# A top-2 mixture of experts on one core: six fixed blocks per expert, or five in twos with shared half blocks

## The chip, the cores and the metric

The kernel runs on one core of a Trainium2 chip. The metric is the device time in microseconds (us) of one execution. Work is done by TensorE (PE in the profile, its weight loads PEld), VectorE (DVE), ScalarE (ACT), GpSimd (POOL) and by DMA queues, most of which SyncE (SP) issues.

## The reference, cut to what matters

Two layers over 2708 tokens of 256 channels, float32. Each layer is a graph attention over an adjacency matrix followed by a feed-forward part; in layer 0 this holds a causal attention too. Both end in a mixture of 8 experts, of which every token uses its best two:

```python
probs = softmax(flat @ router_w.T)              # (2708, 8)
tp, ti = top_k(probs, 2); tp = tp / (tp.sum(-1) + 1e-9)
for e in range(8):                              # hidden width 682
    hh = silu(flat @ w1[e].T) * (flat @ w3[e].T)
    out = out + weights[:, e:e+1] * (hh @ w2[e].T)
```

That is 5416 pairs of token and expert in each layer. How many of them an expert gets depends on the data; the mean is 677.

## The kernel before, in words

The program is `network`: `first` (graph attention, causal attention, routing of layer 0), `experts_blocks(0)`, `second` (graph attention and routing of layer 1), `experts_blocks(1)`. The routing writes each token's row of 268 floats (channels, token number, 8 gates) to a table `xs` in DRAM by an indirect DMA, once for each of its two experts. Expert e owns the rows from e * CAP on and is filled from the front; rows that nobody writes are those that `clear` has put there before (channels and gates 0, a token number beyond the last).

`experts_blocks` works on fixed blocks of P = 128 rows: NB = 6 for every expert, 768 rows, whether they are full or not. For a block (e, j) `fetch` loads the rows into a tile `xt` (SP's queue), `front` transposes them on PE and ACT copies them back as `xT`. `up` (line 2008) multiplies with w1 and w3: the weights are PE's stationary operand, a chunk of 128 hidden units at a time, and the 128 tokens of `xT` move through. The last 42 of the 682 hidden units of both matrices share one chunk (`REST`, `HIGH`). ACT applies SiLU, DVE the product, and the result `hT` has the hidden units on the partitions. `down` (line 2028) takes `hT` as the stationary operand and lets w2 (256 columns) move through, six chunks into one bank of PSUM `y`. DVE scales with the gate (`ys`), and `add_rows` (line 609) adds the rows to their tokens in DRAM by an indirect DMA on POOL's queue. `down` of a block comes after `up` of the next one, and `front` runs two blocks ahead.

The weights of an expert (some 2.1 MB, six DMAs in `load_expert`, line 1967) lie in one of three `rooms`; the next expert's are loaded while the one before last is no longer needed. The first two experts are loaded before the phase.

Not all blocks are worked in `experts_blocks`. A few whose rows are known to be complete early (`EARLY`) run inside `first` and `second`, and the last two of expert 7 in layer 0 (`LATE`) run at the start of `second`, beside the loading of X: tiles of X up to `LATE_T` are loaded ahead of them, the others after. So 43 blocks are left for the phase of layer 0 and 44 for that of layer 1. At the end, flags tell whether the data fit all these assumptions (`missed`, `counts`); if not, a general version of the network runs again (`network_any`).

Two things set the order of instructions. In `first` and `second` a planner (`Plan`) with durations and due times written by hand issues the steps, each engine in that order. In `experts_blocks` the framework's scheduler puts the instructions in each engine's queue: an instruction goes there when its operands and buffers are free by the scheduler's own reckoning, those that stand first in the code going first. So a queue need not have the order of the code. On the chip each queue is worked in order.

Of the kernel before, what the change touches and what calls it, by code (L numbers as in the profile page):

```python
# [10 lines left out]
F32 = mybir.dt.float32  # L11
# [27 lines left out]
NB = 6  # L39
# [4 lines left out]
LATE, LATE_T = ((7, 4), (7, 5)), 12  # L44
# [101 lines left out]
def adj_ffn_kernel(ctx, tc, x, adj, vecs, bias_rows, tab, w_gnn0, w_gnn1, wqkv, wo,  # L146
# [371 lines left out]
    def some_blocks(add, layer, blocks, fetched, needs, weights, xs, acc, new, named, rank):  # L518

        joins = []  # L520
        for k, (e, j, before) in enumerate(blocks):
# [62 lines left out]
            def join(v=v):  # L584
                add_rows(layer, acc, v["ys"], v["xt"])
# [23 lines left out]
    def add_rows(layer, acc, ys, xt):  # L609

        nc.gpsimd.indirect_dma_start(  # L611
            out=acc[:, :], out_offset=bass.IndirectOffsetOnAxis(ap=xt[:, C:C + 1].bitcast(I32), axis=0),
            in_=ys, in_offset=None, compute_op=ALU.add,
            **(dict(bounds_check=N - 1, oob_is_err=False) if layer else {}))
# [795 lines left out]
    def second(X, XB, xs0, x1, x2, sd, mb, xs, arena, load_weights):  # L1410
# [9 lines left out]
        with ExitStack() as s:  # L1420
# [93 lines left out]
            for a, b in zip((0,) + ends, ends):  # L1514
                loads.append(add("SP", 0.45 * (b - a), lambda a=a, b=b: nc.sync.dma_start(
                    out=X[:, a:b, :], in_=x1[a * P:b * P, :].rearrange("(t p) c -> p t c", p=P)),
                    late, rank=-9.0, lands=2.0 if 0 < a < LATE_T else 14.0 if a == 0 else 7.0))
# [449 lines left out]
    def load_expert(room, w1, w3, w2, e):  # L1967
        cut = NF * P
        a, b, c, d = weights_at(room)
        nc.gpsimd.memset(c, 0.0)  # L1970
        nc.gpsimd.memset(d[:, NF, :], 0.0)
        w1v, w3v = (w[:, e, :].rearrange("(k p) h -> p k h", p=P) for w in (w1, w3))
        nc.sync.dma_start(out=a, in_=w1v[:, :, :cut])
        nc.sync.dma_start(out=b, in_=w3v[:, :, :cut])
        nc.sync.dma_start(out=c[:, :, :REST], in_=w3v[:, :, cut:])
        nc.sync.dma_start(out=c[:, :, HIGH:], in_=w1v[:, :, cut:])
        nc.sync.dma_start(out=d[:, :NF, :], in_=w2[e, :cut, :].rearrange("(k p) c -> p k c", p=P))
        nc.sync.dma_start(out=d[:REST, NF, :], in_=w2[e, cut:, :])

    def experts_blocks(layer, w1, w3, w2, xs, acc, arena):  # L1980
# [4 lines left out]

        with ExitStack() as s:
            keep = s.enter_context(tc.tile_pool(name=f"bkeep{layer}", bufs=1))
            hTs = [keep.tile([P, NHC, P], F32, name=f"hT{i}") for i in range(3)]
            for hT in hTs:
                nc.gpsimd.memset(hT[:, NF, :], 0.0)  # L1990
            rooms = [arena[:, :WE], arena[:, WE:], keep.tile([P, WE], F32, name="room")]

            with tc.tile_pool(name=f"slot{layer}", bufs=2) as sp, \
                    tc.tile_pool(name=f"bpu{layer}", bufs=2, space=PSUM) as pu, \
                    tc.tile_pool(name=f"bpt{layer}", bufs=1, space=PSUM) as pt_:

                def fetch(e, j):
                    xt = sp.tile([P, ROW], F32, tag="xt", name="xt", bufs=5)
                    row = e * CAP + j * P
                    after_all(nc.sync.dma_start(out=xt, in_=xs[row:row + P, :]), xs)  # L2000
                    return xt

                def front(xt):
                    xT = sp.tile([P, KC, P], F32, tag="xT", name="xTs", bufs=3)
                    transpose_row(xT, xt, P, pt_, V_LN2 if layer == 0 else None)
                    return xT

                def up(k, w, xT):

                    pp = pu.tile([P, 3 * GW // P, P], F32, tag="pp", name="pup")  # L2010
                    for n in range(2 * NF + 1):
                        if n < 2 * NF:
                            wn, to = w[n // NF][:, :, n % NF * P:(n % NF + 1) * P], P
                        else:
                            wn, to = w[2], HIGH + REST
                        for c in range(KC):
                            nc.tensor.matmul(pp[:to, n, :], wn[:, c, :], xT[:, c, :],  # L2017
                                             start=(c == 0), stop=(c == KC - 1))
                    hT = hTs[k % len(hTs)]
                    sl = sp.tile([P, NF, P], F32, tag="sl", name="sl")  # L2020
                    nc.scalar.activation(sl, pp[:, :NF, :], AF.Silu)  # L2021
                    nc.vector.tensor_tensor(hT[:, :NF, :], sl, pp[:, NF:2 * NF, :], ALU.mult)  # L2022
                    sr = sp.tile([P, P], F32, tag="sr", name="sr")
                    nc.scalar.activation(sr[:REST], pp[HIGH:HIGH + REST, 2 * NF, :], AF.Silu)
                    nc.vector.tensor_tensor(hT[:REST, NF, :], sr[:REST], pp[:REST, 2 * NF, :], ALU.mult)
                    return hT

                def down(e, w, hT, xt):
                    y = pt_.tile([P, C], F32, tag="y", name="y")
                    for n in range(NHC):  # L2030
                        nc.tensor.matmul(y, hT[:, n, :], w[3][:, n, :], start=(n == 0), stop=(n == NHC - 1))  # L2031
                    ys = sp.tile([P, C], F32, tag="ys", name="ys", bufs=3)
                    nc.vector.tensor_scalar(ys, y, xt[:, C + 1 + e:C + 2 + e], None, ALU.mult)  # L2033
                    add_rows(layer, acc, ys, xt)

                done = [b[:2] for b in EARLY[layer]] + list(() if layer else LATE)
                blocks = [(e, j) for e in range(NE) for j in range(NB) if (e, j) not in done]
                xt = [fetch(*blocks[k]) for k in range(3)]
                nxt = [front(xt[k]) for k in range(2)]
                last = None  # L2040
                for k, (e, j) in enumerate(blocks):
                    if k + 3 < len(blocks):
                        xt.append(fetch(*blocks[k + 3]))
                    if j == (2 if e else 3) and e + 2 < NE:
                        load_expert(rooms[(e + 2) % 3], w1, w3, w2, e + 2)
                    if (e, j) == (2, 0):

                        pc = pt_.tile([P, C], F32, tag="y", name="pc")
                        nc.tensor.matmul(pc[:, :NE], allones, hsum[:, NT, :], start=True, stop=True)
                        nc.vector.tensor_tensor(counts[:, layer, :], pc[:, :NE], part, ALU.subtract)  # L2050

                        tests = [(e, t, (j + 1) * P, ALU.is_lt) for e, j, t in EARLY[layer]]
                        if layer == 0:
                            tests.append((LATE[0][0], LATE_T, LATE[0][1] * P, ALU.is_gt))
                        for i, (e_, t, places, test) in enumerate(tests):
                            at = (i + 1) * NE
                            nc.tensor.matmul(pc[:, at:at + 1], allones, hsum[:, t, e_:e_ + 1], start=True, stop=True)
                            to = i + layer * (FLAGS - len(EARLY[1]))
                            nc.vector.tensor_scalar(missed[:, to:to + 1], pc[:, at:at + 1], float(e_ * CAP + places), None, test)
                    if layer == 1 and (e, j) == (3, 0):  # L2060
                        raise_flag(keep, lambda name: pt_.tile([P, C], F32, tag="y", name=name))
                    xT = nxt[k]
                    we = weights_at(rooms[e % 3])
                    hT = up(k, we, xT)
                    if k + 2 < len(blocks):
                        nxt.append(front(xt[k + 2]))
                    if last is not None:
                        down(*last)
                    last = (e, we, hT, xt[k])
                down(*last)  # L2070
# [59 lines left out]
    counts = resid.tile([P, 2, NE], F32, name="counts")  # L2130
    missed = resid.tile([P, FLAGS], F32, name="missed")
# [5 lines left out]
    def raise_flag(fp, bank):  # L2137
        bad = fp.tile([P, 8, NT], F32, name="bad")
        for row in (3, 6, 7):
            nc.vector.memset(bad[:, row, :], 0.0)  # L2140
        nc.vector.tensor_copy(bad[:, 7, :FLAGS], missed)
        nc.vector.tensor_scalar(bad[:, 6, :2 * NE].rearrange("p (a e) -> p a e", a=2), counts, float(NB * P),
                                None, ALU.is_gt)
        nc.vector.tensor_scalar(bad[:, 0, :], norms, BOUND, None, ALU.is_gt)
# [75 lines left out]
```

## Time and profile before

| | |
|---|---|
| median of 3 runs | 1554.26 us (1552.09 to 1555.1) |
| the profiled execution | 1553.19 us, its span 1551.5 us |
| mean granted TensorE clock | 0.982 |
| PE busy | 1468.3 us (95%) in 8988 instructions |
| PE weight loads busy | 1153.4 us (74%) |
| DVE, ACT, POOL busy | 740.9, 551.9, 533.0 us |
| read from and written to DRAM | 87.38 and 61.55 MB |

The span is the time from the first to the last instruction; 1.7 us of the execution lie around it. A line of the timeline gives the start in us, the time that a run of like instructions took, the engine, the line of the kernel, the operation, the tiles written and read, shapes, and how many there were; in brackets stands the idle time before and what ended it. Shapes of a matmul are contraction rows * stationary columns, then partitions x moving columns.

### The profile page before, as it was taken

What the parts mean: (1) busy time and instruction counts of PE and PEld (TensorE: products, weight loads), DVE (VectorE), ACT (ScalarE), POOL (GpSimd) and SP (SyncE); (2) the same over time, 40 slices, a digit from 0 to 9 for tenths busy, and PEclk for the clock granted to TensorE, in tenths of its full rate; (3) what the DMA queues carried; (4) which work ended last, traced back from release to release, by engine and by line L of the source; (5) the groups of instructions that cost most, each with busy time, mean ns of one, the idle gap of its engine ahead of it and who ended that gap; (6) DMA issues with size and microseconds to landing.
All of it is one profiled execution on the core that took longest, in us unless ns stands there. A gap on an engine that the chain in (4) does not pass through costs nothing. (4 is left out here: it accounts for less than half of the span.)

```text
span 1551.5 us, 23359 instructions
## 1 busy us (share of the span) xinstructions
PE 1468.3 (95%) x8988; PEld 1153.4 (74%) x8988; DVE 740.9 (48%) x1450; ACT 551.9 (36%) x1068; POOL 533.0 (34%) x695
## 2 busy tenths in 40 slices
PE   6878899999999999999999899999999999999995
PEld 5633433433437899999999678888778999999995
DVE  6688999966685122222221554867753222222221
ACT  3577766754544111111111453443332111111110
POOL 6677679681163222222222300030444222222221
PEclk9899999999999999999999999999999999999998
DMA  7689767620013332333222850541414333332211
GB/s 261 214 274 316 238 231 252 193 67 8 7 54 94 96 75 53 90 90 90 36 36 33 177 117 1 132 111 61 149 58 109 79 87 88 74 87 50 34 34 17
DMA packets 168029, 165.68 MB, mean 107 GB/s; under 512 B 81384, under 2 KB 148264, under 8 KB 165200
## 3 DMA queue, kind: packets, MB, share of 16 engines
q1 hardware_dynamic: 142582, 134.26, 28.5%
q0 software_dynamic: 21056, 26.24, 9.9%
q10 hardware_dynamic: 4270, 3.58, 0.7%
q8 instruction: 73, 1.20, 0.3%
q14 instruction: 48, 0.39, 0.1%
HBM read 87.38 MB, written 61.55 MB: 96 GB/s over the span
## 5 line engine op out<-in xcount | busy, mean ns | idle before, releaser
L2017 PEld LDWEIGHTS pup<-xTs,arena 128*128 128x128 f32 x2772 | 319.2, 191 | 3.7 <-ACT xTs L283 0.7
L2017 PE MATMUL pup<-xTs,arena 128*128 128x128 f32 x2772 | 321.2, 276 | 0.5 <-ACT xTs L283 0.5
L2022 DVE TENSOR_TENSOR hT<-sl,pup 128x640 f32<-128x640 f32 x87 | 71.5, 821 | 451.4 <-ACT sl L2021 451.4
L2021 ACT ACTIVATE sl<-pup 128x640 f32<-128x640 f32 x87 | 61.2, 703 | 504.5 <-PE pup L2017 499.3
L1578 PE MATMUL po<-hb,PT 128*128 128x257 f32 (+2 forms) x968 | 225.9, 388 | 3.7 <-DVE PT L1571 3.7
L1578 PEld LDWEIGHTS po<-hb,PT 128*128 128x128 f32 (+2 forms) x968 | 176.3, 188 | 42.6 <-issue 11.6
L2031 PE MATMUL y<-arena,hT 128*128 128x256 f32 x756 | 173.8, 380 | 0.6 <-DVE ys L2033 0.6
L1100 ACT ACTIVATE e<-stt 128x1024 f32<-128x1024 f32 (+1 forms) x132 | 125.4, 986 | 93.4 <-PE stt L1094 69.0
L1139 DVE TENSOR_TENSOR es<-es,e 128x1024 f32<-128x1024 f32 x104 | 138.0, 1327 | 29.4 <-ACT e L1100 22.9
L2031 PEld LDWEIGHTS y<-arena,hT 128*128 128x128 f32 x756 | 138.8, 190 | 17.2 <-DVE ys L2033 1.0
L611 POOL DMA_INDIRECT out<-ys,xt x44 | 68.3, 1553 | 231.1 <-DVE ys L2033 228.1
L611 POOL DMA_INDIRECT acc<-ys,xt x43 | 67.1, 1560 | 225.8 <-DVE ys L2033 223.9
L1094 PE MATMUL stt<-qT,kT 64*128 64x512 f32 (+1 forms) x528 | 132.9, 614 | 4.6 <-ACT e L1100 4.5
L1805 POOL DMA_INDIRECT xs<-XR,place x88 | 93.7, 1065 | 92.2 <-DVE mk L1565 41.2
L2017 PE MATMUL pup<-xTs,room 128*128 128x128 f32 (+1 forms) x1056 | 123.8, 276 | 0.0
L2017 PEld LDWEIGHTS pup<-xTs,room 128*128 128x128 f32 (+1 forms) x1056 | 121.9, 190 | 1.2
L1120 PE MATMUL o<-e,V 128*64 128x512 f32 (+1 forms) x528 | 122.4, 586 | 0.0
L1556 ACT ACTIVATE E<-sb,dcol 128x768 f32<-128x768 f32 (+1 forms) x88 | 75.1, 858 | 104.4 <-DVE PT L1571 104.0
L1094 PEld LDWEIGHTS stt<-qT,kT 64*128 64x128 f32 x528 | 44.6, 187 | 77.2 <-issue 62.1
L1120 PEld LDWEIGHTS o<-e,V 128*64 128x64 f32 x528 | 32.9, 136 | 68.6 <-issue 52.6
L2033 DVE TENSOR_SCALAR ys<-y,xt 128x256 f32<-128x256 f32 x87 | 42.1, 484 | 54.2 <-PE y L2031 54.2
L2031 PE MATMUL y<-room,hT 128*128 128x256 f32 x288 | 66.1, 379 | 0.0
(275 smaller groups left out, 1922.0 us busy)
## 6 DMA issues: line engine op xcount, KB each, us to landing
arena<-in_adj SPq DMA_DIRECT2D x21, 1354.0 KB, 7.9
arena<-in_w SPq DMA_DIRECT2D x36, 640.0 KB, 4.6
mb<-mb SPq DMA_DIRECT2D x44, 352.0 KB, 2.4
xs<-none SPq DMA_DIRECT2D x16, 804.0 KB, 11.1
xt<-xs SPq DMA_DIRECT2D x87, 134.0 KB, 2.1
room<-in_w SPq DMA_DIRECT2D x12, 640.0 KB, 5.5
acc<-X SPq DMA_DIRECT2D x21, 128.0 KB, 1.7
out<-X SPq DMA_DIRECT2D x21, 128.0 KB, 1.7
```

The source lines that it names most:

```text
L611: nc.gpsimd.indirect_dma_start(out=acc[:, :], out_offset=bass.IndirectOffsetOnAxis(ap=xt[:, C:C + 1].bitcast(I32), axis=0), in_=ys, in_off ...
L1094: nc.tensor.matmul(st[:r, g, c0(sb):], kT[a:b, sb * P:sb * P + r], qT[a:b, t0 + (sb == t0 + 1):t0 + 2, :, :], start=True, stop=True)
L1100: nc.scalar.activation(e[:r, :, c0(sb):], v[sb, "st"][:r, :, c0(sb):], AF.Exp, scale=1.0 / HD ** 0.5)
L1120: nc.tensor.matmul(v["o"][g * HD:(g + 1) * HD, c:], V[:r, sb, g * HD:(g + 1) * HD], v[sb][:r, g, c:], start=(n + i == 0), stop=(n + i == t ...
L1139: nc.vector.tensor_tensor(es, es, v[sb][:r, :, c:], ALU.add)
L1556: nc.scalar.activation(e[:q, :n], sb[:q, i0:i1], AF.Exp, bias=dcol[:q, j:j + 1], scale=SLOPE - 1.0)
L1578: nc.tensor.matmul(v["po", i][:r, :F], v["PT", j][:q, a:a + r], hb[:q, j, :], start=(j == 0), stop=(j == NT - 1))
L1805: i = nc.gpsimd.indirect_dma_start(out=xs[:, :], out_offset=bass.IndirectOffsetOnAxis(ap=at, axis=0), in_=src, in_offset=None)
L2017: nc.tensor.matmul(pp[:to, n, :], wn[:, c, :], xT[:, c, :], start=(c == 0), stop=(c == KC - 1))
L2021: nc.scalar.activation(sl, pp[:, :NF, :], AF.Silu)
L2022: nc.vector.tensor_tensor(hT[:, :NF, :], sl, pp[:, NF:2 * NF, :], ALU.mult)
L2031: nc.tensor.matmul(y, hT[:, n, :], w[3][:, n, :], start=(n == 0), stop=(n == NHC - 1))
```

## The change

- `NB` is 5: five fixed blocks per expert, 640 rows. They are worked in units of two (`fetch`, `front`, `up`, `down` take a list): `up` moves 256 columns (two blocks) through each stationary chunk of weights and hands each chunk to ACT and DVE by itself; `down` runs five chunks of each block and then the rest chunk of both, the second on partitions 64 and up, with w2's last rows loaded twice for it. The fifth block of an expert is a unit alone.
- Rows beyond 640 go in half blocks of 64 rows, ten for all experts together (`MORE`). `table` works out on DVE from the counts whose they are and where they begin. Two half blocks make one unit: one on partitions 0 to 63, the other on 64 to 127, with the weights of their experts in two more rooms, loaded by register (`register`, `bass.ds`). There the tokens are the stationary operand (64 columns each) and the weights move; `turn_halves` transposes the result one unit later, and `down_halves` follows another unit later. Their units stand ahead of the experts 2 to 6, and after each but the last the two rooms are loaded anew.
- `clear` writes rows 512 to 1024 of an expert, not 0 to 768. A room that has been in use is not zeroed again. `xt` has nine buffers, not five; PSUM has five banks for `up`, two for `y`.
- `LATE` is the blocks 3 and 4 of expert 7, not 4 and 5, and `LATE_T` 10, not 12; the planner's landing times of three X loads differ.
- The flags ask for 512 to 960 rows per expert and at most ten half blocks.

So `experts_blocks` has 35 blocks (14 units of two, 7 of one) and 5 shared units in layer 0, and 36 blocks (15 and 6) and 5 shared units in layer 1.

```diff
-NB = 6
+NB = 5
+HALF_B = 64
+MORE = 10
+LEAST, MOST = 512, 960
-LATE, LATE_T = ((7, 4), (7, 5)), 12
+LATE, LATE_T = ((7, 3), (7, 4)), 10
...
     def clear(xs, e):
-        nc.sync.dma_start(out=xs[e * CAP:e * CAP + NB * P, :].rearrange("(b p) c -> p b c", p=P),
-                          in_=none.unsqueeze(1).to_broadcast([P, NB, ROW]))
+        at, n = e * CAP + LEAST, MOST + HALF_B - LEAST
+        nc.sync.dma_start(out=xs[at:at + n, :].rearrange("(b p) c -> p b c", p=P),
+                          in_=none.unsqueeze(1).to_broadcast([P, n // P, ROW]))
...
-    def load_expert(room, w1, w3, w2, e):
+    def load_expert(room, w1, w3, w2, e, used=False):
-        nc.gpsimd.memset(c, 0.0)
-        nc.gpsimd.memset(d[:, NF, :], 0.0)
+        if not used:
+            nc.gpsimd.memset(c, 0.0)
+            nc.gpsimd.memset(d[:, NF, :], 0.0)
...
+            w1v, w3v = (w[:, bass.ds(e, 1), :].rearrange("(k p) o h -> p k (o h)", p=P) for w in (w1, w3))
+            w2v = w2[bass.ds(e, 1)].rearrange("o h c -> (o h) c")
...
+        for q in (0, HIGH):
+            nc.sync.dma_start(out=d[q:q + REST, NF, :], in_=w2v[cut:, :])
...
+                        if e is None:
+                            for h in range(2):
+                                row = register(tab[0:1, 1, j + h:j + h + 1], NE * CAP - HALF_B)
+                                after_all(nc.sync.dma_start(out=xt[h * HALF_B:(h + 1) * HALF_B, :],
+                                                            in_=xs[bass.ds(row, HALF_B), :]), xs)
...
+                def up(k, w, xT, B):
+                    for n in range(NHC):
+                        pp = pu.tile([P, 2, 2, P], F32, tag="pp", name="pup")
...
+                                nc.tensor.matmul(pp[:to, i, :B, :], wn[:, c, :], xT[:, c, :B, :],
+                                                 start=(c == 0), stop=(c == KC - 1))
...
+                def down(e, w, hT, xts):
+                    ys = [bank() for _ in xts]
+                    for b, y in enumerate(ys):
+                        for n in range(NF):
+                            nc.tensor.matmul(y, hT[:, n, b, :], w[3][:, n, :], start=(n == 0), stop=False)
+                    for b, y in enumerate(ys):
+                        part_ = slice(HIGH * b, HIGH * (b + 1)) if len(ys) > 1 else slice(0, P)
+                        nc.tensor.matmul(y, hT[part_, NF, b, :], w[3][part_, NF, :], start=False, stop=True)
...
+                def up_halves(w, xT, xt, pair):
+                    big, gate, both = (pu.tile([P, 2 * C], F32, tag="pp", name="pup") for _ in range(3))
+                    cut = (NF - 1) * P
+                    for to, at, i, a, b in ((big, 0, 0, 0, cut), (both, 0, 0, cut, cut + P), (both, P, 1, cut, cut + P),
+                                            (both, 2 * P, 2, 0, HIGH + REST), (gate, 0, 1, 0, cut)):
                         for c in range(KC):
+                            for q, wh in zip(halves, w):
+                                nc.tensor.matmul(to[q, at:at + b - a], xT[:, c, 0, q], wh[i][:, c, a:b],
+                                                 start=(c == 0), stop=(c == KC - 1))
...
+                def down_halves(w, hT, xt, gk):
+                    y = bank()
                     for n in range(NHC):
+                        for q, wh in zip(halves, w):
+                            nc.tensor.matmul(y[q, :], hT[:, n, 0, q], wh[3][:, n, :], start=(n == 0), stop=(n == NHC - 1))
...
+                    add_rows(acc, yw[halves[0]], xt[:HALF_B, C:C + 1], layer)
+                    add_rows(acc, yw[halves[1]], upper[:HALF_B], layer)
...
+                for e in range(NE):
+                    left = [(e, j) for j in range(NB) if (e, j) not in done]
+                    if 2 <= e < 2 + MORE // 2:
+                        units.append([(None, 2 * (e - 2))])
+                    units += [left[i:i + 2] for i in range(0, len(left), 2)]
...
+                    if k == 2 or k > 2 and units[k - 3][0][0] is None and more_asked < MORE:
+                        for room in more_rooms:
+                            load_expert(room, w1, w3, w2, register(tab[0:1, 0, more_asked:more_asked + 1], NE - 1), more_asked > 1)
+                            more_asked += 1
+                    if k + 2 < len(units):
+                        xt.append(fetch(units[k + 2]))
...
+                    for f, *args in downs.get(k, ()):
+                        f(*args)
```

More of the change, by code (lines that the diff above doesn't have):

```diff
@@ L584, in join @@
             def join(v=v):
-                add_rows(layer, acc, v["ys"], v["xt"])
+                add_rows(acc, v["ys"], v["xt"][:, C:C + 1], layer)
             r = rank + k
@@ L2037, in experts_blocks @@
[L2037 to L2050, printed above, removed]
+                        for q, wh in zip(halves, w):
+                            nc.tensor.matmul(y[q, :], hT[:, n, 0, q], wh[3][:, n, :], start=(n == 0), stop=(n == NHC - 1))
@@ new lines, in experts_blocks @@
+                own = keep.tile([P, MORE // 2, NE], F32, name="mown")
+                tab = keep.tile([P, 2, MORE], I32, name="mtab")
+                pc = bank()
+                nc.tensor.matmul(pc[:, :NE], allones, hsum[:, NT, :], start=True, stop=True)
+                nc.vector.tensor_tensor(counts[:, layer, :], pc[:, :NE], part, ALU.subtract)
+                done = [b[:2] for b in EARLY[layer]] + list(() if layer else LATE)
+                units = []
+                for e in range(NE):
[3 more added lines that the diff above has]
+                    units += [left[i:i + 2] for i in range(0, len(left), 2)]
@@ new lines, in experts_blocks @@
+                xt = [fetch(u) for u in units[:2]]
+                nxt = [front(x) for x in xt[:2]]
+                asked, more_asked = 1, 0
+                turns, downs = {}, {}
+                for k, unit in enumerate(units):
+                    e = unit[0][0]
+                    if k == 0 or e is not None and e + 2 < NE and asked < e + 2 and units[k - 1][0][0] == e:
+                        asked += 1
+                        load_expert(rooms[asked % 3], w1, w3, w2, asked, asked > 2)
+                    if k == 1:
+                        table()
+                    if k == 2 or k > 2 and units[k - 3][0][0] is None and more_asked < MORE:
[4 more added lines that the diff above has]
+                        xt.append(fetch(units[k + 2]))
+                    if unit[0] == (2, 2):
+                        pc = bank()
@@ L2055, in experts_blocks @@
                         for i, (e_, t, places, test) in enumerate(tests):
-                            at = (i + 1) * NE
-                            nc.tensor.matmul(pc[:, at:at + 1], allones, hsum[:, t, e_:e_ + 1], start=True, stop=True)
+                            nc.tensor.matmul(pc[:, i:i + 1], allones, hsum[:, t, e_:e_ + 1], start=True, stop=True)
                             to = i + layer * (FLAGS - len(EARLY[1]))
[L2059 to L2065, printed above, removed]
+                            nc.vector.tensor_scalar(missed[:, to:to + 1], pc[:, i:i + 1], float(e_ * CAP + places), None, test)
+                    if layer == 1 and unit[0] == (3, 0):
+                        raise_flag(keep, lambda name: bank())
+                    if e is None:
+                        we = [weights_at(room) for room in more_rooms]
+                        hid, gk = up_halves(we, nxt[k], xt[k][0], unit[0][1] // 2)
+                        turns[k + 1] = (k, hid, we, xt[k][0], gk)
+                    else:
+                        we = weights_at(rooms[e % 3])
+                        hT = up(k, we, nxt[k], len(unit))
+                        downs.setdefault(k + 1, []).append((down, e, we, hT, xt[k]))
+                    if k in turns:
+                        of, hid, we, x, gk = turns[k]
+                        downs.setdefault(k + 1, []).append((down_halves, we, turn_halves(of, hid), x, gk))
+                    if k + 2 < len(units):
                         nxt.append(front(xt[k + 2]))
[L2067 to L2070, printed above, removed]
+                    for f, *args in downs.get(k, ()):
+                        f(*args)
+                for f, *args in downs[len(units)]:
+                    f(*args)
     dram = ctx.enter_context(tc.tile_pool(name="dram", bufs=1, space=bass.MemoryType.DRAM))
```

163 lines of the change are left out of this document (125 added, 38 removed).

## The prediction

> **What bounds the kernel now.** I read busy time by stretch first, then the timeline of one block, then the waits. The change lives in the two expert phases (508 to 846 us and 1194 to 1536 us), so these rows decide (span; busy us of PE, PEld, DVE, ACT, POOL; PEclk, DMA share, GB/s):
>
> ```profile
> core 0: us, PE busy (x) PEld busy (x) DVE busy (x) ACT busy (x) POOL busy (x), PEclk, DMA share, GB/s
> 600.00:700.00 100.00, 100.00 (x754) 95.99 (x753) 20.59 (x39) 19.39 (x52) 21.47 (x17) 1.00 0.35 78
> 1300.00:1400.00 100.00, 100.00 (x755) 96.02 (x754) 20.46 (x42) 15.73 (x38) 21.39 (x17) 1.00 0.36 83
> ```
>
> PE never pauses, at a granted clock of 1.00; the others are a fifth busy, the DMA engines a third. In 500 to 850 us PE waited three times in all:
>
> ```profile
> PE pt L278 <- DMA xt<-xs: 1.7, 1, 1.7
> PE pup L2017 <- ACT xTs L283: 0.5, 1, 0.5
> ```
>
> So in these phases time is the number of PE instructions by their spacing. The timeline of one block (start, us, instructions):
>
> ```profile
> 625.83 5.06 PE L2017 MATMUL pup<-xTs,arena 128*128 128x128 f32 x44
> ...
> 630.73 0.38 PE L278 MATMUL pt<-ident,xt 128*128 128x128 f32 x2
> ...
> 630.95 2.76 PE L2031 MATMUL y<-room,hT 128*128 128x256 f32 x12
> ...
> 633.54 0.72 PE L2017 MATMUL pup<-xTs,arena 128*128 128x128 f32 x5
> ```
>
> A float32 matmul is two instructions (22 give x44). From start to start: 44 of 128 columns take 4.90 us, 111.4 ns each; 2 transposes 0.22; 12 of 256 columns 2.59, 215.8 ns each. A block is 7.71 us; 43 + 44 blocks are 670.8 us.
>
> The attention stage shows matmuls in halves of the array side by side:
>
> ```profile
> 330.58 1.94 PE L1120 MATMUL o<-e,V 128*64 128x512 f32 x8
> 332.44 1.99 PE L1094 MATMUL stt<-qT,kT 64*128 64x512 f32 x8
> 334.36 1.98 PE L1020 MATMUL pm<-wq_sb,hTt 128*128 128x512 f32 x4
> 336.27 1.94 PE L1120 MATMUL o<-e,V 128*64 128x512 f32 x8
> ```
>
> Eight half-array instructions take 1.86 us (column halves) or 1.92 (row halves), four of the whole array 1.91: two halves cost one whole. At 215.8 / 256 ns a column four of 512 would be 1.73, so a group pays 0.13 to 0.19 us, I take 0.19, for going into another tiling and out.
>
> **The change, part by part.**
>
> Pairs. `up` has 44 instructions of 256 columns for two blocks: 9.50 us, before 9.80. `front` 0.44 as before. `down` 20 x 0.2158 = 4.32, and the rest chunk as two row halves side by side, 2 x 0.2158 + 0.19 = 0.62. A pair is 14.88 us against 15.42, 0.54 less. Layer 0 has 14 pairs and 7 singles, layer 1 15 and 6. A single stays 7.71.
>
> For pairs the Trainium skill promises more: its page "TensorE: Matmul & The Clock Gate", section Back-to-back issue gap, gives 81 ns a matmul at 128 columns and 131 at 512, so a pair's `up` would need far less than twice a block's. The rows above (111.4 and 215.8 ns) say nearly twice, and I go by them.
>
> Shared units. `up_halves`: 5 groups x 2 chunks x 2 passes = 20 side-by-side slots: 8 of 512 at 0.432, 8 of 128 at 0.111, 4 of 106 at 0.11, 4.79 us, with the tiling 4.98. `turn_halves` 6 transposes 0.66, `front` 0.22, `down_halves` 12 x 0.2158 + 0.19 = 2.78. Together 8.64 us, ten times.
>
> Sum: 29 x 14.88 + 13 x 7.71 + 10 x 8.64 = 618.1 us, **52.7 less**.
>
> A rule of the Trainium skill speaks against this: "TensorEngine Tiling (Array Packing)", section Key Properties, says that changing the tiling mode drains TensorE. The excess of 0.19 us a group agrees in kind; if each of the 98 switches laid bare the whole 380 ns of a 256-wide instruction in place of its 216, that would be 16 us where my terms hold 9.
>
> Scatter-adds. The tail shows their spacing:
>
> ```profile
> 1533.38 2.86 PE L2031 MATMUL y<-arena,hT 128*128 128x256 f32 x12 [0.58 <-DVE ys L2033]
> 1533.60 1.55 POOL L611 DMA_INDIRECT out<-ys,xt  x1 [5.94 <-DVE ys L2033]
> ...
> 1538.19 1.55 POOL L611 DMA_INDIRECT out<-ys,xt  x1 [3.04 <-issue]
> ```
>
> Each waits for the one before to land: 4.6 us apart. Inside a phase that hides: 7 adds an expert cycle (5 blocks, 2 halves) are 32 us beside 8.64 + 2 x 14.88 + 7.71 = 46 us of PE. At the end it shows. With T the end of the last pair's `down`, its adds start at T + 0.6 and T + 5.2, and the last single's, whose matmuls end at T + 3.1, at T + 9.8: 6.7 us after PE. Before it was 1.95 us (PE ends at 1536.24). **+4.7** at the end, and as much ahead of the X load that opens `second`; there 15.4 us of late blocks cover part (PE waited 4.9 us behind that load before): 0 to 4.7, I take **+3**.
>
> Output banks. `down_halves` comes straight after a pair's `down` and needs a bank that DVE is still reading; the 0.58 us above is that wait. 10 x 0 to 0.58: **+3**.
>
> Weights. Ten more experts a layer, 2.1 MB each. SP's rows show an old load threaded between fetches:
>
> ```profile
> 620.54 0.38 SPq L1973 DMA_DIRECT2D room<-in_w  x1
> 622.98 0.32 SPq L2000 DMA_DIRECT2D xt<-xs  x1
> 623.39 0.39 SPq L1974 DMA_DIRECT2D room<-in_w  x1
> ...
> 630.85 0.34 SPq L2000 DMA_DIRECT2D xt<-xs  x1
> 633.30 0.37 SPq L1977 DMA_DIRECT2D room<-in_w  x1
> ```
>
> The code issues a load in one piece; the queue has its pieces where their buffers come free, with fetches between. A load alone moved from 491 to 499 us:
>
> ```profile
> GB/s 0 0 0 0 82 92 133 195 287 328 399 410 410 410 410 410 348 399 369 397 283 203 179 194 215 73 0 66 209 340 356 373 385 385 352 189 29 0 0 0
> ```
>
> 8 us each, three a cycle, 24 of 46 us: room enough, and the w1 and w3 pieces have some 35 us between one shared unit and the next. Register loads (one TENSOR_LOAD of the flag on SP: 487 ns), four a cycle, lie on an SP that mostly waits. Cost from 0 (all hidden) to the second rival's price; I take 0.5 us per cycle, **+4** with the phases' slower start (four blocks to fetch ahead).
>
> What waits behind an SP instruction that blocks is the next fetch, and behind that PE's transposes.
>
> The rest. `table`, some 20 small DVE instructions, lies beside 15 us of the first pair on a DVE a fifth busy; bare it would be 4 us a layer. Per-chunk SiLU and product (256 columns, by the 484 ns of L2033) fit within a chunk's 1.73 us. Dropped `load_expert` memsets free POOL, which is not late. `clear` writes 4 rather than 6 blocks an expert: DVE waited 18.8 us on `X<-hd,ix` in that stage, some of it for bandwidth; 0 to -5, **-1**. LATE's earlier tiles: 0, +-3.
>
> From the profiled execution's 1553.2 (span 1551.5): -52.7 + 4.7 + 3 + 3 + 4 - 1 = -39, so 1514.2; the median of runs is 1.1 above that execution: **1515 us**.
>
> **Rivals.**
>
> Scatter-adds become the bound (faster still). More weight traffic slows them: landing was 3.6 to 5.4 us, with 0.8 for the hand-over (4.6 less the median 3.8) 6.2 at worst, and 6.6 each fills the cycle. At 7.0 a cycle is 49 us, +2.8 x 12 cycles = 34: **1549**. With partial weight waits of 2 to 3 us at ten reloads (+20, 1535) I give this family 0.18.
>
> Slower: SP's queue keeps the order of the code. Then the last piece of a room's load waits for `down_halves`, and behind it stand the second room's load and the next pair's fetch. From there: 1.4 us to start (490.14 to some 491.5 in the load above), 2 for the piece (497 to 499), 8 for the room, 1 for the rows, 12.4; PE has only a single's `up`, 4.9, to do before the transposes: 7.5 us, four times. At the first load two rooms stand ahead: 20.4 less 9.5. That is 41 us a layer, +82: **1597**. It decides from 39 / 10 = 3.9 us per reload. For it: SP did stand at a load's first piece, waiting for `pup`, up to 19.9 us; against: the threaded rows. Chance 0.13, with all prices from 42 us up.
>
> Slower too: column halves with different weights run one after the other: (4.79 + 2.59) x 10 = +74, 1589. L1120's two halves also differ in both operands and ran side by side: 0.03.
>
> It does not do what it says: an expert over 960 rows, or over ten half blocks, would run the network again, above 3000 us. Routing the reference's inputs by its own formulas gives 598 to 745 rows an expert and 8 half blocks in each layer: nil.
>
> **Numbers.** Likeliest case 0.62 (1504 to 1526). Range 1503 to 1550: it adds the first rival. A measurement of this kernel tells 0.2%, 3.1 us. Faster 0.8, within 0.04 (rivals' prices that land there), slower 0.16.
>
> **What would show it.** `up` of a pair at 44 instructions 216 ns apart; shared units with slots of two half-array instructions, some 5 us for `up_halves`; PE near 100% in both phases, which shrink by some 26 us each; last scatter-adds 4.6 us apart after PE's end. I am wrong if PE shows waits of several us for `xt`, `more` or `room` near shared units, if spacing in `up_halves` is twice as wide, or if scatter-adds hold `xt` so long that fetches come late.

## The result and the profile after

The changed kernel takes 1555.16 us (median of 20 runs, 1547.01 to 1560.91); the kernel before, run beside it, takes 1552.66 us (1550.25 to 1556.18). The ratio is 1.0012, 95% interval 1.0000 to 1.0024: no gain of the 39 us that were forecast, and at most 0.24% slower. The profiled execution of the changed kernel took 1552.57 us, its span is 1550.8 us, and the mean granted clock is 0.970 where it was 0.982.

The two stretches that were shown of the kernel before, by windows (span; busy us of PE, PEld, DVE, ACT, POOL; granted clock, DMA share, GB/s), in the changed kernel:

```profile
core 0: us, PE busy (x) PEld busy (x) DVE busy (x) ACT busy (x) POOL busy (x), PEclk, DMA share, GB/s
600.00:700.00 100.00, 94.57 (x548) 75.99 (x548) 22.59 (x68) 21.16 (x60) 21.28 (x14) 0.98 0.58 162
1300.00:1400.00 100.00, 95.17 (x550) 76.37 (x549) 22.92 (x70) 19.23 (x52) 21.18 (x14) 0.98 0.56 158
```

PE was at 100.00 in both; now 5 of 100 us are idle, and the clock is below 1.00 for part of the rest. The DMA engines went from a third to over a half. PE's waits in 500 to 850 us say for whom it stands (total, times, longest):

```profile
PE pup L2061 <- DVE hT L2066: 7.5, 3, 3.9
PE up L558 <- ACT xTs L543: 7.3, 1, 7.3
PE pt L2041 <- DMA xt<-xs: 6.8, 1, 6.8
PE y L2133 <- DVE ys L2086: 0.8, 5, 0.2
```

Before, the rows were 1.7 us for `xt` at the start, 0.5 for `xTs`, and 4.9 us at the layer switch just behind this window. New is the first row: inside `up`, PE waits for DVE, an engine a fifth busy. The work between the waits is nearly as long as it was forecast. The timeline of a shared unit between a pair's `down` and the next pair:

```profile
609.25 4.48 PE L2080 MATMUL y<-room,hT 128*128 128x256 f32 x20
613.67 0.70 PE L2083 MATMUL y<-room,hT 64*128 64x256 f32 x4
614.30 4.89 PE L2099 MATMUL pup<-more,xTs 128*64 128x512 f32 x40
619.12 0.66 PE L2041 MATMUL pt<-ident,xt 128*128 128x128 f32 x4
619.62 2.32 PE L2080 MATMUL y<-room,hT 128*128 128x256 f32 x10
621.77 0.59 PE L2083 MATMUL y<-room,hT 128*128 128x256 f32 x2
622.21 8.80 PE L2061 MATMUL pup<-xTs,arena 128*128 128x256 f32 x40
```

From start to start: `down` of a pair 4.42 us and its rest chunk 0.63, `up_halves` 4.82 (forecast 4.98). The last row is 40 of a pair's 44 instructions; the other 4 came after a wait. A cycle without such a wait (1443.5 to 1490.6 us) takes 47.1 us; the forecast for it was 46, and 46.8 with its terms for a bank and for the weights.

The account by stages, cut where PE ends the routing and where it ends the last `down` (us of one profiled execution each; the first wait of a phase belongs to the phase; the first stage, which the experiments leave as it is, differs by up to 4.5 us among the last four rows, so a single figure is good to some us):

| kernel | first stage | phase 0 | second stage | phase 1 | after PE's end | span |
|---|---|---|---|---|---|---|
| before | 507.0 | 338.0 | 347.6 | 343.7 | 15.2 | 1551.5 |
| after | 505.2 | 333.3 | 351.0 | 341.6 | 19.7 | 1550.8 |
| late_gate | 504.0 | 321.2 | 354.9 | 328.8 | 20.0 | 1528.8 |
| late_sp | 508.5 | 319.3 | 343.6 | 321.5 | 19.7 | 1512.7 |
| late_sp_tail | 506.7 | 317.3 | 343.0 | 320.2 | 16.1 | 1503.3 |

The phases should have shrunk by some 26 us each; they shrank by 4.7 and 2.1. The last three rows are experiments.

### The profile page after: what moved, and what is told of

It reads as the page before. It is cut to its first block, busy times and chain, and to the rows that moved or that the text cites. A ratio compares the mean times of both kernels' runs of the same rounds, so it can differ in the third digit from the quotient of the medians.

```text
span 1550.8 us, 21255 instructions
## 1 busy us (share of the span) xinstructions
PE 1430.0 (92%) x7488; PEld 1025.5 (66%) x7488; DVE 760.8 (49%) x1670; ACT 566.8 (37%) x1134; POOL 530.9 (34%) x687
## 5 line engine op out<-in xcount | busy, mean ns | idle before, releaser
L2061 PE MATMUL pup<-xTs,arena 128*128 128x256 f32 (+2 forms) x1320 | 257.9, 354 | 10.3 <-DVE hT L2066 9.6
L2061 PEld LDWEIGHTS pup<-xTs,arena 128*128 128x128 f32 (+1 forms) x1320 | 220.8, 191 | 43.5 <-DVE hT L2066 11.2
L2065 ACT ACTIVATE sl<-pup 128x256 f32<-128x256 f32 (+1 forms) x210 | 73.2, 350 | 393.5 <-PE pup L2061 359.9
L2066 DVE TENSOR_TENSOR hT<-sl,pup 128x256 f32<-128x256 f32 (+1 forms) x210 | 77.6, 379 | 203.5 <-ACT sl L2065 197.3
L2080 PE MATMUL y<-arena,hT 128*128 128x256 f32 x510 | 115.2, 380 | 1.1 <-DVE ys L2086 1.1
L2061 PE MATMUL pup<-xTs,room 128*128 128x256 f32 (+3 forms) x528 | 104.3, 354 | 5.5 <-DVE hT L2066 5.5
L2086 DVE TENSOR_SCALAR ys<-y,xt 128x256 f32<-128x256 f32 x71 | 31.7, 480 | 152.6 <-PE y L2083 152.5
L2080 PEld LDWEIGHTS y<-arena,hT 128*128 128x128 f32 x510 | 94.7, 190 | 13.7 <-DVE ys L2086 1.9
L2061 PEld LDWEIGHTS pup<-xTs,room 128*128 128x128 f32 (+1 forms) x528 | 87.3, 193 | 19.0 <-DVE hT L2066 6.3
L971 DVE MAX8 tops<-arena 128x8 f32<-128x2708 f32 (+1 forms) x22 | 65.3, 2969 | 1.2 <-DMA arena<-in_adj 1.2
```

What stands on the lines that cost most here:

```text
L2061: nc.tensor.matmul(pp[:to, i, :B, :], wn[:, c, :], xT[:, c, :B, :], start=(c == 0), stop=(c == KC - 1))
L2065: nc.scalar.activation(sl[:, :B, :], pp[:, 0, :B, :], AF.Silu)
L2066: nc.vector.tensor_tensor(hT[:, n, :B, :], sl[:, :B, :], pp[:, 1, :B, :], ALU.mult)
L2080: nc.tensor.matmul(y, hT[:, n, b, :], w[3][:, n, :], start=(n == 0), stop=False)
```

## Where the time went: the theory

As the rows below show it, DVE works its queue in order. The framework's scheduler had put the gate of the next shared unit (`gj`, line 2111, and the copied indices `upper`, line 2138) ahead of the products (line 2066) of the `up` that runs. The gate needs only `own` (the table of whose each half block is) and the rows `xt` of that unit, not its matmuls. On the chip these rows come late, and while DVE waits for them the products of a `up` that has nothing to do with them wait too. One such place in the timeline of the changed kernel:

```profile
667.72 1.42 POOL L614 DMA_INDIRECT acc<-ys,upper  x1 [5.10 <-DMA acc<-ys,xt]
...
670.38 8.80 PE L2061 MATMUL pup<-xTs,arena 128*128 128x256 f32 x40
670.59 0.48 DVE L2086 TENSOR_SCALAR ys<-y,xt 128x256 f32<-128x256 f32 x1 [2.48 <-PE y L2083]
674.71 1.57 POOL L614 DMA_INDIRECT acc<-ys,xt  x1 [5.58 <-DMA arena<-in_w]
678.57 1.50 SPq L2023 DMA_DIRECT2D xt<-xs  x2
...
682.20 0.17 DVE L2111 SCALAR_TENSOR_TENSOR gj<-mown,xt 128x8 f32<-128x8 f32 x1 [11.13 <-DMA xt<-xs]
...
682.59 1.75 DVE L2066 TENSOR_TENSOR hT<-sl,pup 128x256 f32<-128x256 f32 x5
...
683.06 2.04 PE L2061 MATMUL pup<-xTs,arena 128*106 128x256 f32 x4 [3.88 <-DVE hT L2066]
```

Read from below: PE stood 3.88 us for DVE; DVE did five products at once at 682.59, since it had stood 11.13 us for `xt`; SP asked for these rows only at 678.57, when the scatter-add of 674.71 had landed and freed a buffer; and that add came 7.0 us after the one before, beside the loading of weights, where the closing adds of the kernel before were 4.6 apart. SP's waits (505 to 840 us) name the same (line 1518 is the X load that opens the next stage):

```profile
SPq L2027 <- DMA acc<-ys,xt: 139.5, 19, 21.1
SPq L1518 <- DMA acc<-ys,xt: 60.8, 1, 60.8
SPq L2023 <- DMA acc<-ys,xt: 23.0, 4, 7.7
```

A wait of SP for an add is no loss in itself: in the kernel before, SP waited 224.9 us for adds in the same stretch, 38 times, and PE stood 2.2 us in all. Nor is every wait of DVE one of PE. In the changed kernel and in sp_only below, twelve waits of `gj` from 8.4 to 11.1 us each left PE idle for the wait less 7.2 to 7.4 us; those up to 6.9 us left nothing. PE has five banks of PSUM to run ahead in, at 1.73 us a chunk.

What an idle PE costs does not end with the wait. The same place by windows:

```profile
670.00:680.00 10.00, 9.18 (x43) 7.74 (x41) 0.48 (x1) 1.15 (x3) 2.40 (x2) 1.00 0.53 149
680.00:683.00 3.00, 0.00 (x0) 0.00 (x0) 0.74 (x5) 0.00 (x0) 0.73 (x1) 0.92 0.76 153
683.00:686.00 3.00, 2.94 (x10) 2.33 (x11) 1.76 (x7) 1.10 (x4) 1.56 (x1) 0.51 1.02 368
```

After the stall the granted clock is 0.51 for 3 us. Over both phases the six stalls are 7.5 + 7.6 = 15.1 us, and behind four of them the clock is at half for 3.4, 3.4, 3.4 and 6.8 us, which is at most 8.5 us of lost work, as 1.9 us of these stretches lie before PE resumes: some 23 us together.

Two more losses lie outside the units. At a phase's start PE waits 6.8 and 6.2 us for its first rows (before 1.7 us in layer 0; in layer 1 it waited 0.6 us there, for DVE), and the clock is at half for 10.2 us from inside each wait on (before 3.4 us in layer 0, none in layer 1). SP holds the first fetch for a scatter-add of the routing stage's early blocks, which has nothing to do with these rows: "SPq L2027 <- DMA acc<-ys,XR" for 4.0 us in 480 to 520 us. Before, the fetch waited only for the rows themselves (`xs`). So the row buffers seem to lie in memory which that add still reads. At the layer switch PE waits 7.3 us.

Theory A: three separate losses, (1) the place of the gate, (2) the memory of the slots' buffers (row buffers, transposed rows, hidden products and outputs, which the framework takes from one pool of on-chip memory), (3) the closing pair. Rivals: the traffic of the reloaded weights costs by itself; or the wait only moves when one of them is cured.

## Experiments

Times are medians; the experiments ran in three batches on three chips, and the kernel before, run beside each batch, was at 1552.9 to 1556.7 us. A ratio is to that kernel. So a difference between the medians of two batches can be off by up to 4 us.

**late_gate.** The gate and the indices are worked out after the unit's transposes, into `hid`, which is not free earlier:

```diff
-                    gj = sp.tile([P, NE], F32, tag="gj", name="gj")
...
+                def gate_halves(hid, xt, pair):
+                    gk = sp.tile([P, 1], F32, tag="gk", name="gk")
+                    nc.vector.scalar_tensor_tensor(hid[:, :NE], own[:, pair, :], 1.0, xt[:, C + 1:C + 1 + NE],
+                                                   ALU.mult, ALU.mult, accum_out=gk)
+                    upper = hid[:HALF_B, NE:NE + 1]
...
-                        downs.setdefault(k + 1, []).append((down_halves, we, turn_halves(of, hid), x, gk))
+                        hT = turn_halves(of, hid)
+                        downs.setdefault(k + 1, []).append((down_halves, we, hT, x, *gate_halves(hid, x, pair)))
```

> The gate of a shared unit and the copy of its upper token numbers write into hid after its transposes, so that they cannot be put ahead of that; nothing else differs from the changed kernel. Theory A (the scheduler puts these two DVE instructions ahead of the products of the unit before, where they wait for the next shared unit's rows, whose fetch waits for scatter-adds; DVE stands, the PSUM banks stay full, PE stands and its clock drops): DVE's wait for xt of up to 11 us is gone, the six waits of PE for hT inside up (15 us) and the four clock drops behind them (8 us) go, 1555 becomes about 1532. Theory B (weight traffic itself starves PE): DVE's wait moves to the products or to a DMA, and the time stays at 1555 within 4.

Measured: 1531.49 us, ratio 0.984 (0.981 to 0.987), 23.7 us less than the changed kernel (26 by the two ratios); the two phases of the table are 24.9 us shorter. The waits of DVE for `xt` are gone, and so are PE's waits inside `up`:

```profile
600.00:700.00 100.00, 99.70 (x608) 80.80 (x605) 24.93 (x74) 22.48 (x64) 24.39 (x16) 1.00 0.60 165
1300.00:1400.00 100.00, 99.70 (x581) 81.40 (x580) 25.07 (x74) 20.76 (x56) 22.73 (x15) 1.00 0.65 185
```

PE is busy at clock 1.00 beside a DMA share as high as in the changed kernel. SP still waits for the adds (127.7 us at line 2027, 25.3 at line 2023): the late fetch stays, and it harms nobody once no engine waits for it in the wrong place.

**xt14.** Fourteen row buffers in place of nine (`bufs=14` at `xt`), and nothing else.

> Fourteen row buffers, not nine; nothing else. Theory A: the next shared unit's fetch no longer waits for scatter-adds to free a buffer, lands early, and the gate that stands ahead of the products finds its rows there: the stalls of PE inside up shrink from 15 us to under 5, 1555 becomes about 1536. Theory B (traffic): no change, 1555 within 4.

Measured: 1534.25 us, 0.985 (0.983 to 0.988). The gate stays in its place, and DVE's waits for it in layer 0 fall from 31.4 to 7.5 us, the longest from 11.1 to 3.3; PE has no gap inside `up`. So the other end of the chain, the buffer, cures it as well.

**no_reload.** The two rooms of the shared units are loaded once per layer; four of the five shared units then multiply with weights of other experts.

```diff
-                    if k == 2 or k > 2 and units[k - 3][0][0] is None and more_asked < MORE:
+                    if k == 2 or k > 2 and units[k - 3][0][0] is None and more_asked < 2:
```

> The two rooms of the shared units are loaded once a phase and never again, so that four of the five shared units work with the wrong experts' weights; 34 MB less are loaded. Theory A: scatter-adds are 4.6 us apart again where they are 6.5 to 7 now, buffers come free sooner, the gate's wait on DVE shrinks to a few us and PE's stalls to under 5 us: about 1537; the waits that are left are still the gate's. Theory B (SP's queue and weight traffic starve PE directly): all stalls inside the phases go, about 1530, and DVE waits for nothing.

Measured: 1538.68 us, 0.989 (0.987 to 0.992). The adds from 650 to 673 us are 4.2 to 5.3 us apart, where the changed kernel has 4.5 to 7.0 from 654 to 684; DVE still waits 25.2 us for `gj` in layer 0, and up to 8.6 at once (that wait began before its `up` did), but PE has no gap inside `up`: these waits stay near or under the 7.2 us that PE can run ahead, or lie partly before the `up`. Once, in layer 1, PE stood 4.8 us for a flag that DVE worked out behind such a wait. The traffic thus does its harm only through the adds, the buffer and the gate: late_gate keeps all of it and is faster still.

**xt_first.** The row buffers in a pool of their own, opened ahead of the rooms.

> The nine row buffers come from a pool of their own that is opened ahead of the rooms, so that they lie elsewhere in SBUF. Theory A (the larger rooms push the row buffers onto memory that the last early block's scatter-add still reads, so the first fetch of a phase waits for it): first fetches at about 506 and 1186 instead of 509.7 and 1193.4, PE's first waits of 6.8 and 6.2 us shrink to under 2.5, 1555 becomes about 1544. Theory B (the first fetch is late because of the rows' own scatter or the loads ahead of it): first waits and time as they are.

Measured: 1549.81 us, 0.996 (0.995 to 0.998): a small part of what was expected. The wait for rows shrank to 2.0 us, and another came in its place: 3.7 us (layer 0) and 4.2 us (layer 1) for `xTs`, whose buffers, not moved, seem to have stood on that memory still. The stalls inside `up` stayed, as the gate did (15.2 us).

**late_sp.** late_gate, and the whole pool of the slots ahead of the rooms:

```diff
+            sp = s.enter_context(tc.tile_pool(name=f"slot{layer}", bufs=2))
             keep = s.enter_context(tc.tile_pool(name=f"bkeep{layer}", bufs=1))
...
-            with tc.tile_pool(name=f"slot{layer}", bufs=2) as sp, \
-                    tc.tile_pool(name=f"bpu{layer}", bufs=5, space=PSUM) as pu, \
+            with tc.tile_pool(name=f"bpu{layer}", bufs=5, space=PSUM) as pu, \
```

> The gate and the copied indices come late, as in late_gate, and besides that the whole pool of the slots (row buffers, transposed rows, hidden products, outputs) is opened ahead of the pool of the rooms, so that none of its buffers takes memory that the first stage's last scatter-add still reads. Theory A (the wait for rows at the start of each expert phase and the half clock behind it come from that shared memory): the PE waits of 6.8 and 6.0 us at the start shrink to under 2.5 us each, the windows of half clock of 10.2 us near 506 and 1182 us shrink or go, and the time falls from late_gate's 1531.5 to about 1519. Theory B (some other buffer is pushed onto that memory instead, as it was when the row buffers alone were moved, and the wait only gets a new name): about 1531, with as long a first gap on PE.

Measured: 1510.51 us, 0.972 (0.970 to 0.975), 21.0 less than late_gate and 8 less than expected. SP's waits in 480 to 520 us:

```profile
SPq L2027 <- DMA xs<-XR,place: 17.6, 1, 17.6
```

The first fetch now waits only for the write of its own rows; in layer 1 that is 1.5 us, where SP stood 35.4 us in late_gate for an early block's scatter-add (`out<-ys,XR`). PE's first wait is 2.0 us in layer 0, none over 1 us in layer 1, and the half clock behind them is 6.8 and 3.4 us, where it was 10.2 twice. The extra gain is the layer switch: the wait for `xTs` (line 543) fell from 7.6 to 0.3 us, presumably as the buffers there had stood on memory of the slots. Which tiles shared which addresses was not looked up; that the order of the pools decides is shown.

**sp_only** and **before_sp.** The same move on the changed kernel alone, and on the kernel before.

> The changed kernel with the pool of the slots opened ahead of the rooms, and nothing else; the gate stays where it was. Theory A (the stalls inside the units and the waits at the starts and the layer switch are separate losses that add): 1555 less the 21 us that the same move was worth on late_gate = 1534, with the DVE waits for the rows (gj) still at some 30 us per phase and PE gaps inside `up` of 2 to 4 us each. Theory B (one hides in the other: a late start is made up by a shorter stall later, or the other way round): 1543 or more.

> The kernel before with the same pool opened ahead of the rooms. Theory A (the memory that the first stage's last scatter-add still reads got in the way only with the larger rooms of the change; before, PE waited 1.7 us for its first rows in layer 0, under 1 us in layer 1, and 4.9 us at the layer switch): at most those waits and half a short clock window, so 1546 to 1552. Theory B (the move is worth as much here as in the changed kernel): 1532.

Measured: 1533.74 us (0.987, 0.981 to 0.993), and 1555.87 us (0.9998, 0.9984 to 1.0012). The move is worth 21.4 us without the late gate and 21.0 with it, so the two losses add, within the 9 us either way that sp_only's interval leaves (its runs scatter from 1526 to 1546 us). On the kernel before it is worth nothing (0.8 us), no more than the least that theory A allowed: the loss came with the change.

**pairs_only** and **halves_late.** The two halves of the change: the kernel before with its blocks in twos (made from the changed kernel, whose nine row buffers, five banks and `clear` it keeps: `NB = 6`, no half blocks and no rooms for them, 42 pairs); and late_gate with all fixed blocks one at a time.

> The twos alone: the kernel before, with six fixed blocks per expert and full blocks for the rows beyond as it had, but the fixed blocks in twos. Theory A (a pair costs PE some 0.4 to 0.54 us less than two single blocks, and the closing pair delays the last scatter-add): about 42 pairs times 0.44 = -18 us, ends +4 to +5, so about 1541. Theory B (the twos bring no gain of their own, and the cut of the shared rows into halves is what shortens the work): 1553 or more.

> The halves alone, with the gate late: five fixed blocks per expert, all one at a time, and ten half blocks in column halves. Theory A (by unit times: 16 blocks of 7.71 us fewer = -123, ten shared units of 8.6 to 8.8 us more = +87, so -36 on PE; the longer wait at the start of each phase and the half clock behind it give +14 back, slower fetches some 4): about 1536, some 5 us over late_gate, whose 29 pairs save 29 times 0.5 = 15 us but pay some 9 at the two ends. Theory B (single blocks ask for rows and add them evenly, so that nothing waits at the ends, and the twos bring nothing): 1531 or less.

Measured: pairs_only 1556.9 us (1.0025, 1.0012 to 1.0038), halves_late 1527.99 us (0.984, 0.980 to 0.987). Both fell on theory B's side: the twos alone, in the old order of the pools, bring nothing, and taking them out of late_gate makes it 3.5 us faster. The stages say why: pairs_only has 505.4, 331.9, 355.4, 343.5 and 21.7 us. Its phases are 6.1 and 0.2 us shorter than those of the kernel before, the second with 5.9 us of waiting at its start; the second stage is 7.8 longer (PE waits 9.1 us at the switch, with 10.2 us at half clock) and the end 6.5 longer. Ahead of layer 1 SP holds its first fetch 12.0 us for a scatter-add of the early blocks (`out<-ys,XR`), so this loss does not need the two extra rooms; which buffer brings it was not looked up. halves_late has 504.6, 325.5, 347.4, 332.6 and 15.9: against late_gate 4.3 and 3.8 more in the phases, 7.5 and 4.1 less at the ends. So 29 pairs are worth 8.1 us, 0.28 each, and their ends cost 11.6.

**late_sp_tail** and **halves_sp.** late_sp, with the blocks of the last expert one at a time (three pairs fewer in all, not the four that the expectation counts); and late_sp with no pairs.

```diff
-                    units += [left[i:i + 2] for i in range(0, len(left), 2)]
+                    two = 2 if e < NE - 1 else 1
+                    units += [left[i:i + two] for i in range(0, len(left), two)]
```

> As late_sp, and the five blocks of the last expert of each layer go one at a time and not in twos. Theory A (the two scatter-adds of a closing pair stand one behind the other when PE has ended, and the next layer's first transposes and the tail wait for the second): the time from PE's end to the end of the span falls from 19.7 to about 15.3 us, the gap on PE at the layer switch falls from 7.6 to about 5 us, two pairs fewer per layer cost PE 4 times some 0.5 us, and the whole is about 1513 to 1516, some 5 us under late_sp. Theory B (the adds queue up at the end from the shared units before, so the last pair adds nothing): the same as late_sp or 2 us over it.

> As late_sp, with all fixed blocks one at a time: the halves alone, with both repairs. Theory A (a pair is worth 0.28 us of a phase's time, as late_gate against halves_late gives: 8.1 us over 29 pairs, and costs nothing once only the closing one is cut): some 27 times 0.28 = 8 us over late_sp_tail, 1512. Theory B (the twos are worth nothing once nothing waits at the ends): 1504 to 1506.

Measured: late_sp_tail 1504.15 us, ratio 0.968 (0.966 to 0.971): the fastest, 48.7 us under the kernel before. halves_sp 1510.81 us (0.972, 0.969 to 0.974), as fast as late_sp. So the 26 pairs that late_sp_tail keeps are worth 6.7 us (5.3 by the ratios), 0.20 to 0.26 each, and its three undone ones gave 6.4, of which the stages put 4.2 at the ends (3.6 behind PE's end, 0.6 in the second stage). Both agree with theory A, whose 1513 to 1516 for late_sp_tail was counted from a late_sp at 1519. The last scatter-adds of the changed kernel (PE ends at 1531.07):

```profile
1528.44 1.55 POOL L614 DMA_INDIRECT out<-ys,xt  x1 [4.09 <-DVE ys L2086]
1533.32 1.55 POOL L614 DMA_INDIRECT out<-ys,xt  x1 [3.33 <-issue]
1537.73 1.55 POOL L614 DMA_INDIRECT out<-ys,xt  x1 [2.86 <-issue]
```

and those of late_sp_tail, where PE ends at 1487.20:

```profile
1485.42 1.55 POOL L614 DMA_INDIRECT out<-ys,xt  x1 [5.95 <-DVE ys L2086]
1490.21 1.55 POOL L614 DMA_INDIRECT out<-ys,xt  x1 [3.24 <-issue]
```

The last add starts 6.7 us after PE there, 3.0 us here.

**late_sp_tail14.** The same with 14 row buffers.

> As late_sp_tail, with 14 row buffers in place of 9. Theory A (with the gate late nothing that PE needs waits for a row buffer any more, so that five more are idle): 1503 to 1506, the same as late_sp_tail. Theory B (the scatter-adds, slowed beside the weight loads, still hold rows up at times): 1500 or less.

Measured: 1504.99 us, 0.966 (0.964 to 0.968), the same time as late_sp_tail. Once the gate is late, the buffers are no limit.

## Why the prediction was wrong, by its own steps

- **The sum of the units came out, its parts less well.** late_sp_tail, with 26 of the 29 pairs, has phases that are 20.7 and 23.5 us shorter than before: 44.2. By the prediction's terms it is 52.7, less 1.6 for three pairs, 3 for banks and 4 for weights: 44.1. That the two agree so closely is luck. Inside the sum the pairs were sized too high (0.54 against 0.20 to 0.28; by the rows `up` does save 0.3, but `up` of a single block took on average 5.17 us in layer 1 of late_sp_tail and 4.93 in halves_sp, a difference whose cause was not traced), while the output banks (0.15 a unit where 0.3 was taken), `up_halves` (4.82 against 4.98) and the loads, once nothing waits for them in the wrong place, were priced too high, the other way.
- **The step that failed is "Weights", +4.** It looked at whether the loads fit (8 us each, 24 of 46: they do, and late_gate shows PE at 99.70 beside them) and gave a late fetch the price of PE's own transposes. The late fetch did not stand before PE's transposes but before DVE's gate, and cost 15.1 us of stalls and up to 8.5 of clock; late_gate returns 23.7. "What waits behind an SP instruction that blocks is the next fetch" named the queue on SP and stopped there; the next in-order queue, DVE's, was taken as "a fifth busy".
- **"The phases' slower start"**, inside the same +4, and **the layer switch, +3**: together some 21 us of waits and half clock, which the order of the pools returned. The change's effect on where buffers lie was no term of the sum at all. The +3 came out in size (second stage 351.0 against 347.6) by luck: once the pools are reordered, undoing the closing pair, the forecast's reason for it, takes only 0.6 us off that stage (343.6 to 343.0).
- **The first rival was near in time and wrong in mechanism.** It put 1549 on slower adds as the bound. They did slow, to 6.0 to 7.0 us beside loads, and the "wrong if" clause, that adds hold `xt` so long that fetches come late, is what happened. But they bound nothing themselves: late_gate has such spacing too (6.0 to 7.4 us in layer 0), and PE at 99.70.
- **Right:** the closing adds, +4.7 (19.7 against 15.2 us after PE's end); column halves side by side (4.82 us); the queue threaded by buffers, not in the order of the code; spacing of 216 ns.
- The forecast of 1515, less the two ends of 7.7 that late_sp_tail avoids, and with its three pairs back, is 1509; that kernel runs at 1504. So the change can be had at about what was forecast; it lost that to two placements, the gate's and the pools', that were no terms of the sum.

## What to carry to other kernels

When an operation is added to an in-order engine, ask of each of its operands when it comes on the chip, not how busy the engine is: a 0.2 us instruction that is ready early by the scheduler's reckoning can hold back everything behind it for 11 us. Writing its result to a buffer that is busy until its proper place is a way to keep it there. Look after a change of buffer sizes at what the first transfer of a stage waits for, and take the last unit of a stage out of a batching whose results leave one by one.

## What the runs showed of the hardware

- Of PE's stalls inside `up` in the changed kernel, sp_only and xt_first, those up to 2.2 us left the clock alone and those from 2.6 to 3.9 us each came with 3.4 or 6.8 us at half clock; of four in between (2.4 to 2.5 us) three did. Of ten waits of 6.0 to 7.0 us at the phase starts (the changed kernel, late_gate, halves_late, no_reload, xt14) nine came with 10.2 us and one with 6.8. At the start of layer 0, where PE has other short gaps beside, waits of 1.6 to 2.0 us were enough for 3.4 or 6.8 us (before, pairs_only, sp_only, late_sp, late_sp_tail, halves_sp). The Trainium skill, "TensorE: Matmul & The Clock Gate", Part 1, has the clock fall to half after an idle window of some 3.4 us that runs free of the kernel. The lengths agree, being multiples of 3.4 us; the gap that suffices was shorter here, down to 2.4 us inside `up`.
- In the changed kernel scatter-adds that follow one another were 6.0 to 7.0 us apart where weights were loaded at a high DMA share (605 to 618 us, 0.85; 654 to 675 us, 0.78) and 4.5 to 4.8 just behind (623 to 632 us, 0.63; 675 to 684 us, 0.51).
